# A stack of graph attention layers on one core: repeated scores by two DMAs through DRAM and a parametric relu, in place of a matmul and a VectorE pass

## The chip, the core and the metric

One core of a Trainium2 chip. Times are device microseconds of one execution of the whole program, launch not included; the profiled execution has its own time and its own span (first to last instruction). Lower is better.

## What is computed

128 independent graphs of 128 nodes with 512 features go through four layers, each a graph attention with residual and layer normalisation. All attention has the same core: a score per pair of nodes is the sum of a source term and a target term, a leaky relu of slope 0.2 is put on it, non-edges are masked, and a softmax over the source nodes weighs their features. Cut to what matters:

```python
# layer 0: one head
scores = leaky_relu(s_src[:, :, None] + s_dst[:, None, :] + attn_b[0], 0.2)
attn = softmax(where(adj + eye == 0, -inf, scores), axis=-1)
x = layernorm(x + attn @ x)

# layer 1: two stacked attentions, four heads of 256, then one of 512
def gat_layer(x, mask, W, a_src, a_dst, bias, concat):
    xl = (x @ W).reshape(B, N, H, F)
    e = leaky_relu(asrc[:, :, None, :] + adst[:, None, :, :], 0.2)
    attn = softmax(where(mask[..., None], e, NEG_INF), axis=1)
    out = einsum('bsdh,bshf->bdhf', attn, xl)     # heads concatenated, or their mean
    return out + bias
h = elu(gat_layer(x, mask, W1, ..., concat=True))
x = layernorm(x + gat_layer(h, mask, W2, ..., concat=False))

# layer 2: eight heads of 64;  layer 3: one head, elu of the output
```

Everything is float32. Each graph has six calls of the attention core: l0 (1 head), l1 (4), l2 (1), l3 in two halves (4 and 4), l4 (1), fifteen heads in all.

## The kernel before

A generator `graph(g, loaded)` issues the instructions of one graph and yields between steps. The loop at the end keeps a list of active graphs and advances each by one step per tick; a new graph starts every 10 ticks (`STAGGER`), so many graphs are under way at once, each in another layer. The tile framework then puts the instructions of each engine in an order of its own and adds the semaphores; on the engine they run in that order. So a step that waits holds up those of other graphs behind it on the same engine. Tiles come from rotating pools (three buffers each in the working pool, four for the score tile `z` and the transposed weights `pt`), PSUM from eight banks in rotation.

The attention core is `attend` (lines 155 to 215). With nodes on the partitions it needs, on every partition, the row of scores of the other nodes:

- GpSimd multiplies the identity by the column of scores (L160), which gives a diagonal matrix per head, `dg`.
- TensorE multiplies a matrix of ones by it (L167): `pd` in PSUM holds the row of scores on every partition.
- ScalarE adds the partition's own score as a bias and writes `z` to SBUF, one instruction per head (L177).
- VectorE forms the leaky relu as max(0.2 z, z) over all heads (L181), then subtracts per head from the mask and takes the row minimum (L187).
- ScalarE takes the exponential with the row sum (L194); VectorE inverts the sum (L200); TensorE transposes (L208); VectorE copies the transposed weights to SBUF as `pt` (L211).
- Only in l1 (`scaled=True`) GpSimd multiplies the weights by the inverse sums ahead of the transposes (L202).

Around l1: `xl`, the projected features, takes the layer's bias on its way out of PSUM (L305, VectorE, two halves of 512). The output of the four heads is made already transposed: for each of eight blocks of 128 features the weight operand is the block of `xl` and the moving operand the head's `pt` (L318, eight matmuls of 128 columns into two banks). ScalarE takes exponential and relu from each bank (L324, L325), VectorE joins them to the ELU, `hT` (L327). `hT` feeds the second attention's scores (L336) and projection (L344) as it is.

Other lines that the prediction names: L260 (score products of layer 0 on VectorE), L283 and L289 and L299 (copy of the transposed x1, score matmul, projection of l1), L353 (output of l2), L376 (projection of layer 2's heads), L392 (outputs of its halves), L398 (their scaling), L423, L425, L427 and L430 (minimum, exponential, combination and residual of the last ELU), L225 and L226 (GpSimd's part of the normalisation), L228 (its end), L285 (GpSimd, residual plus bias). L108 belongs to the set-up, which runs once. The inputs and the output go over SP's DMA queue, three transfers per graph; the weights come over ScalarE's queue at the start.

Of the kernel before, what the change touches and what calls it, by code (L numbers as in the profile page):

```python
# [8 lines left out]
F32 = mybir.dt.float32  # L9
I32 = mybir.dt.int32  # L10
AF = mybir.ActivationFunctionType
ALU = mybir.AluOpType
AX = mybir.AxisListType

P = 128
# [10 lines left out]
def tile_gat_stack(  # L26
# [117 lines left out]
    io = ctx.enter_context(tc.tile_pool(name="io", bufs=3))  # L144
    wk = ctx.enter_context(tc.tile_pool(name="wk", bufs=3))
    sm = ctx.enter_context(tc.tile_pool(name="sm", bufs=8))

    def load(g):
        xt = io.tile([P, F], F32, tag="x0", name=f"x0_{g}")
# [2 lines left out]
        nc.sync.dma_start(out=at, in_=adj[g])  # L152
        return xt, at

    def attend(g, lay, src, dst, mask, nh, res, scaled=False):


        n = f"{lay}_{g}"
        dg = wk.tile([P, 4, P], F32, tag="diag", name=f"dg_{n}")
        nc.gpsimd.tensor_mul(  # L160
            dg[:, :nh, :],
            ident.unsqueeze(1).to_broadcast([P, nh, P]),
            dst.unsqueeze(2).to_broadcast([P, nh, P]),
        )
        yield
        pd = bank(f"pd_{n}")
        nc.tensor.matmul(  # L167
            pd[:, : nh * P],
            lhsT=ones,
            rhs=dg[:, :nh, :].rearrange("p h j -> p (h j)"),  # L170
            start=True,
            stop=True,
        )
        yield
        z = wk.tile([P, 4, P], F32, tag="z", name=f"z_{n}", bufs=4)
        for h in range(nh):
            nc.scalar.activation(  # L177
                z[:, h, :], pd[:, h * P : (h + 1) * P], AF.Identity, bias=src[:, h : h + 1]
            )
        yield  # L180
        nc.vector.scalar_tensor_tensor(  # L181
            out=z[:, :nh, :], in0=z[:, :nh, :], scalar=SLOPE, in1=z[:, :nh, :],
            op0=ALU.mult, op1=ALU.max,
        )
        nm = sm.tile([P, 4], F32, tag="nm", name=f"nm_{n}")
        for h in range(nh):
            nc.vector.tensor_tensor_reduce(  # L187
                out=z[:, h, :], in0=z[:, h, :], in1=mask, scale=-1.0, scalar=FMAX,
                op0=ALU.add, op1=ALU.min, accum_out=nm[:, h : h + 1],
            )  # L190
        yield
        rs = sm.tile([P, 4], F32, tag="rs", name=f"rs_{n}")
        for h in range(nh):
            nc.scalar.activation(  # L194
                z[:, h, :], z[:, h, :], AF.Exp, bias=nm[:, h : h + 1], scale=-1.0,
                accum_out=rs[:, h : h + 1],
            )
        yield
        ri = sm.tile([P, 4], F32, tag="ri", name=f"ri_{n}")
        nc.vector.reciprocal(ri[:, :nh], rs[:, :nh])  # L200
        if scaled:
            nc.gpsimd.tensor_mul(  # L202
                z[:, :nh, :], z[:, :nh, :], ri[:, :nh].unsqueeze(2).to_broadcast([P, nh, P])
            )
            yield
        pp = bank(f"pp_{n}")
        for h in range(nh):
            nc.tensor.transpose(pp[:, h * P : (h + 1) * P], z[:, h, :], ident)  # L208
        yield
        pt = wk.tile([P, 4, P], F32, tag="pt", name=f"pt_{n}", bufs=4)  # L210
        nc.vector.tensor_copy(  # L211
            pt[:, :nh, :].rearrange("p h i -> p (h i)"), pp[:, : nh * P]
        )
        yield
        res.append((pt, ri))
# [26 lines left out]
    def graph(g, loaded):  # L242
# [53 lines left out]
        for c in range(2):  # L296
            px = bank(f"px1_{g}_{c}")
            for k in range(KF):
                nc.tensor.matmul(  # L299
                    px, lhsT=xT[:, k, :], rhs=w1t[:, k, c * 512 : (c + 1) * 512],  # L300
                    start=(k == 0), stop=(k == KF - 1),
                )

            cols = slice(c * 512, (c + 1) * 512)
            nc.vector.tensor_add(xl[:, cols], px, b1t[:, cols])  # L305
        yield
        yield from attend(g, "l1", sc1[:, H1:], sc1[:, :H1], m1, H1, res, scaled=True)
        pt, ri = res.pop()


        e1 = wk.tile([P, KH, P], F32, tag="e1", name=f"e1_{g}", bufs=2)
        r1 = wk.tile([P, KH, P], F32, tag="r1", name=f"r1_{g}", bufs=2)
        hT = wk.tile([P, KH, P], F32, tag="hT", name=f"hT_{g}", bufs=2)
        for c in range(2):
            pa = bank(f"pa1_{g}_{c}")
            for u in range(4):
                k = 4 * c + u
                nc.tensor.matmul(  # L318
                    pa[:, u * P : (u + 1) * P], lhsT=xl[:, k * P : (k + 1) * P],
                    rhs=pt[:, k * P // FH, :], start=True, stop=True,  # L320
                )
            yield
            cols = slice(4 * c, 4 * c + 4)
            nc.scalar.activation(e1[:, cols, :].rearrange("p k i -> p (k i)"), pa, AF.Exp)  # L324
            nc.scalar.activation(r1[:, cols, :].rearrange("p k i -> p (k i)"), pa, AF.Relu)  # L325
            yield
            nc.vector.scalar_tensor_tensor(  # L327
                out=hT[:, cols, :], in0=e1[:, cols, :], scalar=-1.0, in1=r1[:, cols, :],
                op0=ALU.add, op1=ALU.min,
            )  # L330
        yield


# [146 lines left out]
```

## Time and profile before

| | us |
|---|---|
| median of 3 runs | 4681.03 |
| lowest to highest | 4670.32 to 4681.74 |
| the profiled execution, its time | 4670.32 |
| the profiled execution, its span | 4668.5 |

| engine | busy us | share of the span | instructions |
|---|---|---|---|
| PE (matmuls) | 4325.3 | 93% | 18692 |
| PEld (weight loads, beside PE) | 2605.1 | 56% | 18692 |
| DVE (VectorE) | 3559.1 | 76% | 10952 |
| ACT (ScalarE) | 1928.9 | 41% | 6913 |
| POOL (GpSimd) | 1725.1 | 37% | 2566 |

The 16 DMA engines were busy for about 6% of the span, and the mean granted clock of TensorE was 0.977. The chain of work that ended last is made of TensorE for 43%, VectorE for 41%, GpSimd for 7%, ScalarE for 3%; 5% is issue.

How to read it: a matmul of float32 is two records in the trace. In the groups, the columns are line, engine, operation, out<-in by the program's names, shapes and count, then busy time, mean nanoseconds of one, and idle time ahead of it with what ended it. A name as `z_l` stands for the tile of all layers. "DVE", "ACT", "POOL" and "SP" are VectorE, ScalarE, GpSimd and SyncE. The shares of the whole span are means over 128 graphs in a pipeline; the figures per graph are what counts, and they are had by dividing by 128, or from windows in the steady stretch.

### The profile page before, as it was taken

What the parts mean: (1) busy time and instruction counts of PE and PEld (TensorE: products, weight loads), DVE (VectorE), ACT (ScalarE), POOL (GpSimd) and SP (SyncE); (2) the same over time, 40 slices, a digit from 0 to 9 for tenths busy, and PEclk for the clock granted to TensorE, in tenths of its full rate; (3) what the DMA queues carried; (4) which work ended last, traced back from release to release, by engine and by line L of the source; (5) the groups of instructions that cost most, each with busy time, mean ns of one, the idle gap of its engine ahead of it and who ended that gap; (6) DMA issues with size and microseconds to landing.
All of it is one profiled execution on the core that took longest, in us unless ns stands there. A gap on an engine that the chain in (4) does not pass through costs nothing.

```text
span 4668.5 us, 61210 instructions
## 1 busy us (share of the span) xinstructions
PE 4325.3 (93%) x18692; PEld 2605.1 (56%) x18692; DVE 3559.1 (76%) x10952; ACT 1928.9 (41%) x6913; POOL 1725.1 (37%) x2566
## 2 busy tenths in 40 slices
PE   1999999999999999999999999999999999999997
PEld 0555555555555555555555555555555555555554
DVE  5577777777777777777777777777777777777777
ACT  0344444444444444444444444444444444444443
POOL 1333333333333333333333333333333333333332
PEclk9999999999999999999999999999999999999998
DMA  2000000000000000000000000000000000000000
GB/s 89 9 16 19 16 18 18 16 16 18 19 16 18 19 16 18 18 17 18 19 17 16 18 19 16 18 19 16 18 18 17 16 18 19 16 18 19 16 10 16
DMA packets 63142, 88.15 MB, mean 19 GB/s; under 512 B 10816, under 2 KB 27200, under 8 KB 62816
## 3 DMA queue, kind: packets, MB, share of 16 engines
q1 hardware_dynamic: 55296, 75.52, 5.0%
q10 hardware_dynamic: 7520, 8.72, 0.6%
q8 instruction: 151, 2.47, 0.2%
q14 instruction: 175, 1.43, 0.1%
HBM read 50.66 MB, written 33.55 MB: 18 GB/s over the span
## 4 chain that ended last, share of the span: by engine, by line
PE 43%; DVE 41%; POOL 7%; issue 5%; ACT 3%; ACTq 0%; DMA 0%; POOLq 0%; SPq 0%; DVEq 0%
PE px L299 21%; DVE z_l L187 7%; PE pc L336 5%; DVE x L228 4%; DVE z_l L181 4%; DVE y L427 4%; DVE st_n L220 3%; DVE pt_l L211 3%; PE pp_l L208 3%; POOL rd_n L226 3%; PE pc L289 3%; POOL z_l L202 3%; PE pa L318 3%; PE pd_l L167 2%; PE pa L392 2%
## 5 line engine op out<-in xcount | busy, mean ns | idle before, releaser
L194 ACT ACTIVATE z_l<-z_l,nm_l 128x128 f32<-128x128 f32 x1920 | 765.3, 406 | 1083.1 <-DVE nm_l L187 1082.8
L299 PE MATMUL px<-w1t,x1T 128*128 128x512 f32 x2048 | 985.4, 638 | 0.0
L344 PE MATMUL px<-w2t,hT 128*128 128x512 f32 x2048 | 919.7, 602 | 0.0
L160 POOL TENSOR_TENSOR dg_l<-ident,sc 128x128 f32<-128x128 f32 (+1 forms) x768 | 663.0, 876 | 668.9 <-PE pd_l L167 394.1
L225 POOL TENSOR_SCALAR rd_n<-mv_n 128x1 f32<-128x1 f32 x512 | 116.1, 227 | 1735.4 <-DVE mv_n L222 1360.5
L187 DVE CUSTOM_DVE_ANT_0 z_l<-z_l,m 128x128 f32<-128x128 f32 x1920 | 673.9, 384 | 4.6
L299 PEld LDWEIGHTS px<-w1t,x1T 128*128 128x128 f32 x2048 | 405.5, 203 | 477.4 <-issue 477.4
L177 ACT ACTIVATE z_l<-pd_l,sc 128x128 f32<-128x128 f32 x1920 | 585.8, 378 | 162.0 <-PE pd_l L167 159.4
L344 PEld LDWEIGHTS px<-w2t,hT 128*128 128x128 f32 x2048 | 382.1, 192 | 432.6 <-issue 432.6
L167 PE MATMUL pd_l<-dg_l,ones 128*128 128x128 f32 (+1 forms) x1536 | 523.4, 436 | 14.8 <-POOL dg_l L160 14.8
L181 DVE SCALAR_TENSOR_TENSOR z_l<-z_l 128x128 f32<-128x128 f32 (+1 forms) x768 | 477.5, 622 | 5.8 <-ACT z_l L177 5.8
L376 PE MATMUL px<-wht,x2T 128*128 128x512 f32 x1024 | 471.0, 603 | 0.0
L228 DVE TENSOR_SCALAR x<-x,mv_n,rd_n 128x512 f32<-128x512 f32 x384 | 209.1, 545 | 320.4 <-POOL rd_n L226 320.4
L211 DVE COPY pt_l<-pp_l 128x128 f32<-128x128 f32 (+1 forms) x768 | 370.0, 482 | 84.5 <-PE pp_l L208 84.4
L305 DVE TENSOR_TENSOR xl<-px,b1t 128x512 f32<-128x512 f32 x256 | 176.5, 689 | 291.5 <-PE px L299 291.5
L194 ACT ACTIVATION_READ_ACCUMULATOR z_l<-z_l,nm_l 128x1 f32 x1920 | 385.4, 201 | 0.0
L208 PE MATMUL pp_l<-ident,z_l 128*128 128x128 f32 x1920 | 321.2, 275 | 18.7 <-ACT z_l L194 11.0
L289 PE MATMUL pc<-wc,x1T 128*128 128x8 f32 x1024 | 136.9, 260 | 210.5 <-ACT x1T L283 210.0
L324 ACT ACTIVATE e<-pa 128x512 f32<-128x512 f32 x256 | 153.1, 598 | 412.4 <-PE pa L318 412.4
L208 PEld LDWEIGHTS pp_l<-ident,z_l 128*128 128x128 f32 x1920 | 237.4, 145 | 124.4 <-issue 96.2
L226 POOL TENSOR_TENSOR rd_n<-rd_n,neghalf 128x1 f32<-128x1 f32 x512 | 291.7, 570 | 32.5
L392 PEld LDWEIGHTS pa<-xl,pt_l 128*128 128x128 f32 x2048 | 260.5, 193 | 66.0 <-issue 58.4
(78 smaller groups left out, 6449.6 us busy)
## 6 DMA issues: line engine op xcount, KB each, us to landing
x<-in_x_dram SPq DMA_DIRECT2D x128, 256.0 KB, 2.6
out_dram<-y SPq DMA_DIRECT2D x128, 256.0 KB, 2.0
adj<-in_adj_dram SPq DMA_DIRECT2D x128, 64.0 KB, 1.8
w1t<-in_L_gnn_W_dram ACTq DMA_DIRECT2D x1, 2048.0 KB, 11.2
w2t<-in_L_gnn_W_dram ACTq DMA_DIRECT2D x1, 2048.0 KB, 16.2
wht<-in_L_gnn_W_dram ACTq DMA_DIRECT2D x8, 128.0 KB, 5.5
b1t<-in_L_gnn_b_dram ACTq DMA_DIRECT2D x1, 512.0 KB, 6.3
a<-in_L_gnn_att_src_dram ACTq DMA_DIRECT2D x1, 512.0 KB, 5.6
```

The lines of the kernel that those rows point to most:

```text
L160: nc.gpsimd.tensor_mul(dg[:, :nh, :], ident.unsqueeze(1).to_broadcast([P, nh, P]), dst.unsqueeze(2).to_broadcast([P, nh, P]),)
L167: nc.tensor.matmul(pd[:, : nh * P], lhsT=ones, rhs=dg[:, :nh, :].rearrange("p h j -> p (h j)"), start=True, stop=True,)
L177: nc.scalar.activation(z[:, h, :], pd[:, h * P : (h + 1) * P], AF.Identity, bias=src[:, h : h + 1])
L181: nc.vector.scalar_tensor_tensor(out=z[:, :nh, :], in0=z[:, :nh, :], scalar=SLOPE, in1=z[:, :nh, :], op0=ALU.mult, op1=ALU.max,)
L187: nc.vector.tensor_tensor_reduce(out=z[:, h, :], in0=z[:, h, :], in1=mask, scale=-1.0, scalar=FMAX, op0=ALU.add, op1=ALU.min, accum_out=nm ...
L194: nc.scalar.activation(z[:, h, :], z[:, h, :], AF.Exp, bias=nm[:, h : h + 1], scale=-1.0, accum_out=rs[:, h : h + 1],)
L208: nc.tensor.transpose(pp[:, h * P : (h + 1) * P], z[:, h, :], ident)
L211: nc.vector.tensor_copy(pt[:, :nh, :].rearrange("p h i -> p (h i)"), pp[:, : nh * P])
L226: nc.gpsimd.tensor_tensor(out=rd, in0=rd, in1=neghalf, op=ALU.pow)
L299: nc.tensor.matmul(px, lhsT=xT[:, k, :], rhs=w1t[:, k, c * 512 : (c + 1) * 512], start=(k == 0), stop=(k == KF - 1),)
L344: nc.tensor.matmul(px, lhsT=hT[:, k, :], rhs=w2t[:, k, :], start=(k == 0), stop=(k == KH - 1))
L376: nc.tensor.matmul(px, lhsT=xT[:, k, :], rhs=wht[:, k].rearrange("p h o -> p (h o)"), start=(k == 0), stop=(k == KF - 1),)
```

## The change

`attend` no longer makes a diagonal matrix and multiplies it by ones. The column of scores of the nodes is written to a row in DRAM by one DMA and read back to all 128 partitions by a second, both on SP's queue; the second must wait for the first. The ScalarE instruction reads that tile in SBUF (with a step of the number of heads), adds the bias and applies the leaky relu in one instruction (Prelu with alpha 0.2). The VectorE pass is gone.

In l1 the weights are no longer scaled ahead of the transposes. The four heads' output is made with nodes on the partitions: the head's `pt` is the weight operand and 256 columns of `xl` the moving one. VectorE scales each head by its inverse sum and adds the bias, from PSUM; the ELU is taken on 1024 columns (minimum, exponential, combination); TensorE transposes the result in eight blocks, and ScalarE and VectorE copy one bank each to `hT`. `xl` leaves PSUM without bias, one half by ScalarE, one by VectorE.

```diff
+    dram = ctx.enter_context(tc.tile_pool(name="dram", bufs=4, space=bass.MemoryType.DRAM))
...
-    def attend(g, lay, src, dst, mask, nh, res, scaled=False):
+    def attend(g, lay, src, dst, mask, nh, res):
...
-        dg = wk.tile([P, 4, P], F32, tag="diag", name=f"dg_{n}")
-        nc.gpsimd.tensor_mul(
-            dg[:, :nh, :],
-            ident.unsqueeze(1).to_broadcast([P, nh, P]),
-            dst.unsqueeze(2).to_broadcast([P, nh, P]),
-        )
-        yield
-        pd = bank(f"pd_{n}")
-        nc.tensor.matmul(
-            pd[:, : nh * P],
-            lhsT=ones,
-            rhs=dg[:, :nh, :].rearrange("p h j -> p (h j)"),
-            start=True,
-            stop=True,
-        )
+        row = dram.tile([P, nh], F32, tag=f"row{nh}", name=f"row_{n}")
+        nc.sync.dma_start(out=row, in_=dst)
+        db = wk.tile([P, P, nh], F32, tag=f"db{nh}", name=f"db_{n}")
+        nc.sync.dma_start(
+            out=db.rearrange("p j h -> p (j h)"),
+            in_=row.rearrange("j h -> (j h)").partition_broadcast(P),
+        )
+        yield
         yield
         z = wk.tile([P, 4, P], F32, tag="z", name=f"z_{n}", bufs=4)
         for h in range(nh):
             nc.scalar.activation(
-                z[:, h, :], pd[:, h * P : (h + 1) * P], AF.Identity, bias=src[:, h : h + 1]
+                z[:, h, :], db[:, :, h], AF.Prelu, bias=src[:, h : h + 1], alpha=SLOPE
             )
         yield
-        nc.vector.scalar_tensor_tensor(
-            out=z[:, :nh, :], in0=z[:, :nh, :], scalar=SLOPE, in1=z[:, :nh, :],
-            op0=ALU.mult, op1=ALU.max,
-        )
...
-        if scaled:
-            nc.gpsimd.tensor_mul(
-                z[:, :nh, :], z[:, :nh, :], ri[:, :nh].unsqueeze(2).to_broadcast([P, nh, P])
-            )
-            yield
...
-            cols = slice(c * 512, (c + 1) * 512)
-            nc.vector.tensor_add(xl[:, cols], px, b1t[:, cols])
+            if c == 0:
+                nc.scalar.copy(xl[:, :512], px)
+            else:
+                nc.vector.tensor_copy(xl[:, 512:], px)
...
-            for u in range(4):
-                k = 4 * c + u
+            for u in range(2):
+                h = 2 * c + u
                 nc.tensor.matmul(
-                    pa[:, u * P : (u + 1) * P], lhsT=xl[:, k * P : (k + 1) * P],
-                    rhs=pt[:, k * P // FH, :], start=True, stop=True,
+                    pa[:, u * FH : (u + 1) * FH], lhsT=pt[:, h, :],
+                    rhs=xl[:, h * FH : (h + 1) * FH], start=True, stop=True,
                 )
             yield
-            cols = slice(4 * c, 4 * c + 4)
-            nc.scalar.activation(e1[:, cols, :].rearrange("p k i -> p (k i)"), pa, AF.Exp)
-            nc.scalar.activation(r1[:, cols, :].rearrange("p k i -> p (k i)"), pa, AF.Relu)
+            for u in range(2):
+                h = 2 * c + u
+                cols = slice(h * FH, (h + 1) * FH)
+                nc.vector.scalar_tensor_tensor(
+                    out=z1[:, cols], in0=pa[:, u * FH : (u + 1) * FH], scalar=ri[:, h : h + 1],
+                    in1=b1t[:, cols], op0=ALU.mult, op1=ALU.add,
+                )
+
+        nc.vector.tensor_scalar_min(t1, z1, 0.0)
+        yield
+        nc.scalar.activation(t1, t1, AF.Exp)
+        yield
+        nc.vector.scalar_tensor_tensor(
+            out=z1, in0=t1, scalar=-1.0, in1=z1, op0=ALU.add, op1=ALU.max
+        )
+        yield
+        for hT, pb, c in transposed(z1, KH, f"h1T_{g}", "hT"):
             yield
-            nc.vector.scalar_tensor_tensor(
-                out=hT[:, cols, :], in0=e1[:, cols, :], scalar=-1.0, in1=r1[:, cols, :],
-                op0=ALU.add, op1=ALU.min,
-            )
+            dst = hT[:, 4 * c : 4 * c + 4, :].rearrange("p k i -> p (k i)")
+            if c == 0:
+                nc.scalar.copy(dst, pb)
+            else:
+                nc.vector.tensor_copy(dst, pb)
```

More of the change, by code (lines that the diff above doesn't have):

```diff
@@ L302, in graph @@
                 )
-            cols = slice(c * 512, (c + 1) * 512)
-            nc.vector.tensor_add(xl[:, cols], px, b1t[:, cols])
+            if c == 0:
+                nc.scalar.copy(xl[:, :512], px)
+            else:
+                nc.vector.tensor_copy(xl[:, 512:], px)
         yield
-        yield from attend(g, "l1", sc1[:, H1:], sc1[:, :H1], m1, H1, res, scaled=True)
+        yield from attend(g, "l1", sc1[:, H1:], sc1[:, :H1], m1, H1, res)
         pt, ri = res.pop()
-        e1 = wk.tile([P, KH, P], F32, tag="e1", name=f"e1_{g}", bufs=2)
@@ L312, in graph @@
-        r1 = wk.tile([P, KH, P], F32, tag="r1", name=f"r1_{g}", bufs=2)
-        hT = wk.tile([P, KH, P], F32, tag="hT", name=f"hT_{g}", bufs=2)
+        z1 = wk.tile([P, HF], F32, tag="z1", name=f"z1_{g}", bufs=2)
+        t1 = wk.tile([P, HF], F32, tag="t1", name=f"t1_{g}", bufs=2)
         for c in range(2):
             pa = bank(f"pa1_{g}_{c}")
-            for u in range(4):
-                k = 4 * c + u
+            for u in range(2):
+                h = 2 * c + u
                 nc.tensor.matmul(
-                    pa[:, u * P : (u + 1) * P], lhsT=xl[:, k * P : (k + 1) * P],
-                    rhs=pt[:, k * P // FH, :], start=True, stop=True,
+                    pa[:, u * FH : (u + 1) * FH], lhsT=pt[:, h, :],
+                    rhs=xl[:, h * FH : (h + 1) * FH], start=True, stop=True,
```

## The prediction, made before the changed kernel ran

> **What bounds the kernel now.** I read the page's busy shares first, then busy time by windows, the waits, the groups by form, the timeline of TensorE and the chain that ended last.
>
> From the answer by windows (columns: length, then busy time and instructions of PE, PEld, DVE, ACT, POOL, then granted clock, DMA share, GB/s):
>
> ```profile
> 1000.00:2000.00 1000.00, 953.00 (x4135) 574.42 (x4134) 772.95 (x2403) 424.28 (x1525) 381.48 (x568) 0.98 0.06 17
> 2000.00:3000.00 1000.00, 951.30 (x4145) 574.54 (x4144) 775.83 (x2404) 424.17 (x1522) 380.48 (x565) 0.98 0.05 18
> 3000.00:4000.00 1000.00, 949.49 (x4117) 571.77 (x4116) 774.25 (x2417) 428.75 (x1542) 381.90 (x567) 0.98 0.06 18
> ```
>
> TensorE is busy 95.1% of the steady stretch. A graph has (18692 - 4)/128 = 146 of its records, so the 12397 records of these 3000 us are 84.9 graphs: one per 35.33 us, with 33.6 us of TensorE and 1.7 us of holes. VectorE follows with 27.4 us. So the kernel is bound by TensorE, and its holes are the second thing to look for. The waits name them:
>
> ```profile
> PE pc L289 <- ACT x1T L283: 210.0, 120, 1.8
> ```
>
> 210.0/128 = 1.64 us per graph: the first matmuls of layer 1 wait for the ScalarE copy of the transposed x1. Apart from one in the set-up, every other wait of PE in that list is below 20 us in total. The chain shows what that hole is the end of:
>
> ```profile
> 2523.85 0.60 DVE z_l L181
> ...
> 2539.73 1.44 DVE y L427
> 2541.17 0.60 DVE z_l L181
> 2541.77 0.60 DVE y L430
> 2542.64 0.28 issue
> 2543.11 0.47 ACT xl L381
> 2543.58 0.50 ACT x1T L283
> 2544.12 1.06 PE pc L289 x8
> ```
>
> For half of each period VectorE works without a pause and the chain runs through it; ScalarE's copy stands behind an exponential that waits for VectorE. L427 is to be noted: 1.44 us for 512 elements.
>
> [...]
>
> ```profile
> L427 DVE SCALAR_TENSOR_TENSOR y<-t,y x128: 681/1515/1517, 277.6 to 4661.8; 128x512 f32<-128x512 f32 x128
> ```
>
> (min/median/max in ns.) In the timeline the one of 1.44 us shown above runs beside a GpSimd L160 of 1087 ns. [...] The trace has one load of 1283 ns; the changed program as built also has just one, so parametric ReLU and exponential share a set.
>
> **The change, part by part, per graph.** Groups by form (busy us, mean ns):
>
> ```profile
> L160 POOL TENSOR_TENSOR dg_l<-ident,sc 128x512 f32<-128x512 f32 x384 | 452.9, 1180 | 115.6 <-DVE sc L294 103.2 <-DVE sc L373 6.5 <-DVE mv_n L222 4.8
> L181 DVE SCALAR_TENSOR_TENSOR z_l<-z_l 128x512 f32<-128x512 f32 x384 | 266.3, 694 | 1.3 <-ACT z_l L177 1.2
> L181 DVE SCALAR_TENSOR_TENSOR z_l<-z_l 128x128 f32<-128x128 f32 x384 | 211.1, 550 | 4.6 <-ACT z_l L177 4.6
> L187 DVE CUSTOM_DVE_ANT_0 z_l<-z_l,m 128x128 f32<-128x128 f32 x1920 | 673.9, 384 | 4.6
> ```
>
> TensorE is costed from start to start in its timeline, because its modelled ends overlap:
>
> ```profile
> 2518.15 0.60 PE L208 MATMUL pp_l<-ident,z_l 128*128 128x128 f32 x4
> 2518.58 1.02 PE L353 MATMUL pa<-xl,pt_l 128*128 128x512 f32 x2
> 2519.45 1.02 PE L167 MATMUL pd_l<-dg_l,ones 128*128 128x512 f32 x2
> ```
>
> - TensorE: the six broadcasts (L167) go: three of 512 columns at 0.86 us and three of 128 at 0.22 (two records of 0.11) = -3.24. Eight transposes of the layer-1 output come: 8 x 0.11 = +0.88. The head outputs (L318, 16 records of 0.11 = 1.78) become 8 records of 256 columns, half of 0.43 each = 1.72. Net -2.4.
> - VectorE: L181 goes, (266.3 + 211.1)/128 = -3.73. L305 and L327, two each at 0.69, -2.76. [...] L427 1.47 to 0.69, -0.78; L187, 15 x (384 - 285, what most of them take in the timeline), -1.49. New: four scalings from PSUM at 0.41 (L398, 256 elements) 1.62; the minimum of 1024, below twice L423's 0.41, 0.75; the ELU's 1024-wide combination 1.22 (L108 has that width[...]); two PSUM copies at 0.68. Sum +4.95. Net -3.8, to about 23.5 us.
> - ScalarE: fifteen biases stay as Prelu, from 0.378 to at most L194's 0.406 (SBUF source; a strided read of four heads is not shown by the trace: I take no surcharge, and bound it at double, 0.35 x 12 = 4.2, on an engine busy 15 us of 35). Two exponentials and two relus of 0.60 go; one 1024-wide exponential (1.06) and two copies (0.59) come: about zero.
> - GpSimd: L160 and L202 go, (663.0 + 133.7)/128 = -6.2 us[...].
> - SP: twelve more DMAs per graph at 0.34 us of issue (the out store's row) = 4.1 us beside three now. Each read must wait on SP for its row to land, and the DMAs behind it wait too: in the built order rows and reads stand in pairs (l2 with l0, l4 with l3's first half, l1 with l3's second), and the out store lies ahead of l1's read.
>
> Transfer times are bounded by these (KB, median us to landing):
>
> ```profile
> out_dram<-y SPq DMA_DIRECT2D x128, 256.0 KB, 2.0
> adj<-in_adj_dram SPq DMA_DIRECT2D x128, 64.0 KB, 1.8
> w0s<-in_L_gnn_attn_w_src_dram ACTq DMA_DIRECT2D x1, 256.0 KB, 3.5
> ac<-in_L_gnn_W_attn_dram ACTq DMA_DIRECT2D x2, 0.1 KB, 4.9
> ```
>
> A row of 4-byte pieces: 2.0 (a store) to 4.9 (single elements in the crowded set-up). A read: 1.8 for one head, 2.6 (the x load) to 3.5 for four, w0s being exactly one 2 KB row repeated on 128 partitions. I take 2.0 + 2.6.
>
> **What hides them.** I walked one period of the built TensorE order, zero at the end of layer 1's last projection. Until 3.5 come seven groups already fed (transposes, l2 and l0 outputs). Then l3's second half waits for VectorE, which first copies the projection and two attention tiles (1.2 us) and masks seven heads at 0.29 (to 3.25), then copies the tile (3.85): a hole of 0.5. Score matmuls and projection of layer 2 end at 14.0, outputs and transposes at 18.8, layer 3's scores and projection at 23.1, layer 1's scores at 24.0, its projection at 31.6. Against this:
> - l2: score at 5.5 to 7, landed by about 12, used by ScalarE at 14.6.
> - l4: score at 17.5, its read held on SP by l3's row until 20, landed by 22.6; used at 23.7, when the copy of layer 3's projection is through.
> - l1, the tightest: score 24.2, row landed 26.5, then the out store holds SP until about 28; landed near 31, used from 32.9.
>
> The 1.64 us hole closes: between the transposes of x1 and its scores now stand half the head outputs, layer 3's scores and projection, 5.2 us. So 33.46 us of TensorE (33.6 by the windows) - 2.42 = 31.04, plus the 0.5 hole, plus 0.55 that I allow for waits that the walk is too coarse for: 32.1 us, 3.23 less. Over 127 periods -410. Fill and drain, with too few graphs to cover a round trip, cost perhaps 7 more attentions of 3.5 us, +25. Span 4668.5 - 385 = 4283.5, and the 1.8 us between span and time of the profiled execution (4670.32) make 4285. That execution is 0.2% below the median, 4681; within the range.
>
> **The rivals.**
> - TensorE all but free of holes: 31.3 us, 4668.5 - 4.03 x 127 + 25 + 2 = about 4185. For it: VectorE keeps 8 us spare. Against: the 0.5 hole is in the order.
> - Round trips partly shown: the upper bounds, 4.9 + 3.5 to 4.1, bring l1's read in about 0.8 late and l4's 2 to 3: 33.3 us, about 4440. For it: SP is in order. Against: the upper rows are from the crowded set-up, the DMA share is 6%.
> - Slower: l1's read lands so late that its four heads hold ScalarE, then VectorE's masking, and with it the tile copy queued behind, for which TensorE waits. It is free until about 33, then a microsecond for a microsecond; it eats the gain when row and read together take about 11.7 us instead of 4.6. At 13 us the period is 36.6 and the time about 4860. Against: no row above comes near.
> - That the edit does less than it says: the built order has no L167 or L181 work left, so this is excluded.
>
> **How the numbers follow.** 0.3% is about what a measurement of this kernel can tell from no change. Forecast 0.62 (4230 to 4340), no holes 0.14, partly shown 0.14 (4340 to 4600), slower or level 0.10. Outside 4180 to 4470 lie about half of the second, a third of the third and the last: 0.2. Faster: the first three less a little, 0.87; within 0.3% 0.03; slower 0.10.
>
> **What would show it.** Right: spacing of graphs near 32 us, no wait of PE for the x1T copy, L427's successor near 0.69 us, VectorE near 23.5 us per graph, reads landing below 3.5 us. Wrong: ScalarE's Prelu waiting for a DMA of the repeated row by over 1 us per graph and PE idle before l3's output; or rows that need over 5 us.

## The result, and the profile after

| | median (range), us | against before |
|---|---|---|
| before | 4675.67 (4670.24 to 4681.74, 4 runs) | |
| after | 5408.89 (5403.92 to 5432.26, 4 runs) | 1.158 [1.154, 1.162] |

The change makes the kernel 15.8% slower; 4285 had been forecast. The profiled execution after took 5410.9 us, with a span of 5409.1.

First the same view by windows as before (length, then busy time and instructions of PE, PEld, DVE, ACT, POOL, then granted clock, DMA share, GB/s):

```profile
1000.00:2000.00 1000.00, 848.82 (x3331) 506.16 (x3331) 594.73 (x2066) 424.55 (x1320) 201.38 (x325) 0.89 0.19 40
2000.00:3000.00 1000.00, 835.82 (x3297) 499.71 (x3297) 589.31 (x2048) 422.01 (x1307) 197.45 (x318) 0.89 0.18 40
3000.00:4000.00 1000.00, 831.17 (x3292) 497.92 (x3290) 588.02 (x2029) 415.57 (x1296) 197.55 (x319) 0.89 0.19 39
```

TensorE is busy 84% instead of 95%, with fewer records to run (134 a graph instead of 146), and its granted clock fell from 0.98 to 0.89. VectorE, ScalarE and GpSimd have all come down or stand still: no engine has become the bound. From the start of one layer-1 projection to the next, which is called TensorE's period below, it is 40.62 us, 5.3 more than before.

Layers are counted by the attention calls here, as in the prediction: the scores, projection and outputs of layer 1 are L275, L285 and L302 of the kernel after, those of layer 2 (the model's second attention of layer 1) L335, L343 and L352, those of layer 3 (the model's layer 2) L367, L375 and L391. The waits say on what the time goes (us in total over 128 graphs, times, longest):

```profile
ACT z_l L172 <- DMA db_l<-row_l: 1088.6, 245, 17.6
...
PE pc L367 <- ACT x2T L363: 733.2, 122, 11.3
```

TensorE's wait for the x1T copy is gone. In its place the score matmuls of layer 3 (L367) wait 733.2/128 = 5.7 us per graph for the copy of the transposed x2, and ScalarE, which makes that copy, waits 8.5 us per graph for the repeated rows. SyncE's own list has the next step back:

```profile
SPq L164 <- DMA row_l<-sc: 1184.1, 430, 9.2
```

The chain that ended last, from 2516 to 2549 us, with what each piece took:

```profile
2516.82 0.17 DVE sc L340
2517.01 0.33 SPq L162
...
2517.39 8.70 DMA row_l<-sc
...
2526.16 4.06 DMA db_l<-row_l
...
2530.61 1.73 ACT z_l L172 x4
2532.34 0.48 ACT x2T L363
...
2532.86 1.89 PE pc L367 x8
2534.75 6.54 PE px L375 x8
2541.29 0.79 PE pc L275 x8
2542.08 6.97 PE px L285 x16
```

In place of VectorE's half of the period stands one round trip: the score of layer 2 (L340) is ready, its row takes 8.7 us to DRAM, the read back 4.1, and then the Prelus and, behind them in ScalarE's order, the copy for layer 3. TensorE in the same stretch (start, duration, and in brackets the idle time ahead):

```profile
2512.69 1.10 PE L391 MATMUL pa<-xl,pt_l 128*128 128x64 f32 x8 [0.58 <-DVE pt_l L197]
...
2526.62 1.03 PE L302 MATMUL pa<-xl,pt_l 128*128 128x256 f32 x4
2532.86 1.89 PE L367 MATMUL pc<-wc,x2T 128*128 128x16 f32 x8 [5.21 <-ACT x2T L363]
2534.59 6.70 PE L375 MATMUL px<-wht,x2T 128*128 128x512 f32 x8
```

Two things are to be seen. The hole of 5.21 us is there, and the eight records of the projection behind it (L375) take 6.70 us. In the kernel before the same eight (L376) took 3.68:

```profile
2499.47 3.68 PE L376 MATMUL px<-wht,x2T 128*128 128x512 f32 x8
```

TensorE runs at about half speed for a while. The view by windows, taken over this stretch of the kernel after, has a granted clock of 0.52:

```profile
2532.90:2541.00 8.10, 8.10 (x16) 4.38 (x17) 4.00 (x13) 3.24 (x9) 0.00 (x0) 0.52 0.20 41
```

The transfers (KB each, median us from issue to landing):

```profile
db_l<-row_l SPq DMA_DIRECT2D x384, 256.0 KB, 4.0
...
db_l<-row_l SPq DMA_DIRECT2D x384, 64.0 KB, 4.7
...
row_l<-sc SPq DMA_DIRECT2D x384, 0.5 KB, 7.9
row_l<-sc SPq DMA_DIRECT2D x384, 2.0 KB, 1.6
```

The smallest transfer is the slowest: a one-head row of 512 bytes takes 7.9 us, a four-head row of four times the bytes 1.6. And the three groups that the prediction spoke of (busy us, mean ns):

```profile
L172 ACT ACTIVATE z_l<-db_l,sc 128x128 f32<-128x128 f32 x1920 | 808.2, 491 | 1450.7 <-DMA db_l<-row_l 1088.6 <-PE pp_l L194 356.6 <-DVE z L310 4.3
...
L178 DVE CUSTOM_DVE_ANT_0 z_l<-z_l,m 128x128 f32<-128x128 f32 x1920 | 547.6, 299 | 450.8 <-ACT z_l L172 399.3
...
L426 DVE SCALAR_TENSOR_TENSOR y<-t,y 128x512 f32<-128x512 f32 x128 | 87.7, 685 | 0.8 <-ACT t L424 0.8
```

### The profile page after: what moved, and what is told of

It is laid out like the page before. It is cut to its first block, busy times and chain, and to the rows that moved or that the text cites. A ratio compares the mean times of both kernels' runs of the same rounds, so it can differ in the third digit from the quotient of the medians.

```text
span 5409.1 us, 58792 instructions
## 1 busy us (share of the span) xinstructions
PE 4380.4 (81%) x17156; PEld 2618.6 (48%) x17156; DVE 3126.1 (58%) x10696; ACT 2185.2 (40%) x6785; POOL 1026.7 (19%) x1670
## 4 chain that ended last, share of the span: by engine, by line
PE 46%; DMA 34%; ACT 12%; DVE 4%; issue 2%; SPq 1%; ACTq 0%; POOL 0%; POOLq 0%; DVEq 0%
DMA row_l<-sc 20%; PE px L285 16%; DMA db_l<-row_l 14%; PE px L375 13%; ACT z_l L172 11%; PE pc L367 4%; PE pc L335 4%; PE pa L391 3%; PE px L343 2%; PE pc L275 2%; DVE pt_l L197 2%; PE pp_l L194 1%; ACT x2T L363 1%; DVE z_l L178 1%; SPq L162 0%
## 5 line engine op out<-in xcount | busy, mean ns | idle before, releaser
L172 ACT ACTIVATE z_l<-db_l,sc 128x128 f32<-128x128 f32 x1920 | 808.2, 491 | 1450.7 <-DMA db_l<-row_l 1088.6
L343 PE MATMUL px<-w2t,h1T 128*128 128x512 f32 x2048 | 951.1, 608 | 0.0
L285 PE MATMUL px<-w1t,x1T 128*128 128x512 f32 x2048 | 912.1, 598 | 0.0
L367 PE MATMUL pc<-wc,x2T 128*128 128x16 f32 x1024 | 234.2, 369 | 733.2 <-ACT x2T L363 733.2
L178 DVE CUSTOM_DVE_ANT_0 z_l<-z_l,m 128x128 f32<-128x128 f32 x1920 | 547.6, 299 | 450.8 <-ACT z_l L172 399.3
L375 PE MATMUL px<-wht,x2T 128*128 128x512 f32 x1024 | 745.4, 895 | 0.0
L367 PEld LDWEIGHTS pc<-wc,x2T 128*128 128x128 f32 x1024 | 222.4, 319 | 782.8 <-ACT x2T L363 781.9
L285 PEld LDWEIGHTS px<-w1t,x1T 128*128 128x128 f32 x2048 | 380.0, 191 | 429.6 <-issue 429.6
L343 PEld LDWEIGHTS px<-w2t,h1T 128*128 128x128 f32 x2048 | 373.2, 192 | 373.2 <-issue 373.2
L375 PEld LDWEIGHTS px<-wht,x2T 128*128 128x128 f32 x1024 | 294.5, 302 | 348.0 <-issue 348.0
L391 PEld LDWEIGHTS pa<-xl,pt_l 128*128 128x128 f32 x2048 | 261.9, 194 | 207.4 <-DVE pt_l L197 147.6
L391 PE MATMUL pa<-xl,pt_l 128*128 128x64 f32 x2048 | 272.9, 277 | 78.1 <-DVE pt_l L197 78.1
L238 POOL TENSOR_SCALAR m<-adj 128x128 f32<-128x128 int32 x256 | 304.1, 1188 | 68.4 <-DVE nm_l L178 29.6
```

What stands on the lines that cost most here:

```text
L172: nc.scalar.activation(z[:, h, :], db[:, :, h], AF.Prelu, bias=src[:, h : h + 1], alpha=SLOPE)
L178: nc.vector.tensor_tensor_reduce(out=z[:, h, :], in0=z[:, h, :], in1=mask, scale=-1.0, scalar=FMAX, op0=ALU.add, op1=ALU.min, accum_out=nm ...
L238: nc.gpsimd.tensor_scalar(out=m, in0=a, scalar1=0.0, scalar2=-BIG, op0=op, op1=ALU.mult)
L285: nc.tensor.matmul(px, lhsT=xT[:, k, :], rhs=w1t[:, k, c * 512 : (c + 1) * 512], start=(k == 0), stop=(k == KF - 1),)
L343: nc.tensor.matmul(px, lhsT=hT[:, k, :], rhs=w2t[:, k, :], start=(k == 0), stop=(k == KH - 1))
L367: nc.tensor.matmul(pc[:, : 2 * H2], lhsT=xT[:, k, :], rhs=wc3[:, k, :], start=(k == 0), stop=(k == KF - 1),)
```

## The experiments

The theory: the one-head rows land late because they are made of 128 pieces of 4 bytes that lie side by side; l2's round trip is then longer than its cover, and TensorE pays twice, with a hole and with half speed after it. Rivals: the new head output moved the work that would have covered it; SyncE's queue is too full, so that transfers wait for the loads and the store; and the order alone is at fault, with the row's write and its read next to each other.

All times against the kernel before on the same chip (4669 to 4676 us there):

| kernel | us | ratio | TensorE's period, us |
|---|---|---|---|
| before | 4676 | | 35.34 |
| after | 5408.9 | 1.158 [1.154, 1.162] | 40.62 |
| e1 16-byte rows | 4587.9 | 0.980 [0.978, 0.983] | 34.64 |
| e2 4-byte rows, steps after the read | 6041.6 | 1.293 [1.291, 1.295] | 45.87 |
| e3 new head output alone | 4496.5 | 0.962 [0.961, 0.963] | 33.84 |
| e4 DMA and Prelu alone | 5613.0 | 1.201 [1.199, 1.203] | 42.33 |
| e6 Prelu alone | 4552.1 | 0.974 [0.972, 0.975] | 34.44 |
| e7 e6, scores as weights | 4568.7 | 0.977 [0.975, 0.979] | 34.42 |
| e8 after, with filler matmuls | 5689.8 | 1.217 [1.211, 1.223] | 42.93 |
| e9 after, loads and store from GpSimd | 5588.1 | 1.197 [1.194, 1.200] | 42.25 |
| e10 16-byte rows and a step | 4053.4 | 0.868 [0.866, 0.869] | 30.29 |
| e11 new head output and Prelu | 4485.8 | 0.961 [0.959, 0.962] | 33.92 |
| e12 e1, loads and store from GpSimd | 4444.6 | 0.951 [0.949, 0.953] | 33.41 |
| e13 4-byte rows and a step | 6015.9 | 1.289 [1.287, 1.291] | 45.75 |
| e15 DMA and Prelu alone, in e10's form | 4058.8 | 0.869 [0.868, 0.871] | 30.35 |

### e1: the rows in pieces of 16 bytes

```
+        if nh == 1:
+            four = sm.tile([P, 4], F32, tag="four", name=f"four_{n}")
+            nc.vector.tensor_copy(four, dst.to_broadcast([P, 4]))
+            dst = four
-        row = dram.tile([P, nh], F32, tag=f"row{nh}", name=f"row_{n}")
+        row = dram.tile([P, 4], F32, tag=f"row{nh}", name=f"row_{n}")
```

(and the tile of the read four wide for one head too.) Every row is now 2 KB, every read 256 KB.

> One-head rows are written as four copies, 16 bytes a piece, and read back as 2 KB rows. Late-row theory: the row lands in about 1.5 us in place of 8, the read in 4; from l2's score to its use there are 6.5 us, so TensorE's hole ahead of layer 3's scores falls from 5.2 to under 1 us, its half-speed stretch goes, and the time is 4250 to 4400. Queue theory (SP's order and its waits): 5300 to 5500, since no place in the queue changes. Load theory (bytes and packets slow every transfer): above 5400, as three reads per graph grow fourfold. Head-output theory (the new layer-1 output is the cost): about 5400.

It measured 0.980 [0.978, 0.983]: four times the bytes for one head, and 821 us less than the change. At 4588 us that is above the 4250 to 4400 of the late-row theory and far below what the rivals had. The longest wait of its TensorE, and its transfers:

```profile
PE pa L356 <- DVE pt_l L201: 326.4, 124, 3.8
```

```profile
db_l<-row_l SPq DMA_DIRECT2D x768, 256.0 KB, 4.5
...
row_l<-four_l SPq DMA_DIRECT2D x384, 2.0 KB, 2.4
row_l<-sc SPq DMA_DIRECT2D x384, 2.0 KB, 2.7
```

The row is down from 7.9 to 2.4 us, the wait ahead of layer 3's scores is gone, and a smaller hole of 326.4/128 = 2.5 us stands ahead of layer 2's outputs (L356). Slow records have moved there with it: the outputs behind a hole of 2.98 us took 2.08 us, behind one of 2.15 us 1.13. So the rows' form is most of the loss, but not all that stood between the change and its forecast.

### e2: more distance behind the read

Three more `yield`s after the read's issue, for one head, rows as in the change.

> The rows keep their 4-byte pieces, but one-head attentions take three more steps between the read's issue and its use. Late-row theory: rows still land in 8 us, but about 10 us more stand in front of the use, so the hole closes and the time is 4250 to 4450. Queue theory: over 5000, since SP's waits stay. Head-output theory: about 5400. Load theory: about 5400 if the engines are the limit.

It became slower still, 6042 us, and missed the 4250 to 4450 of the late-row theory; only the queue theory had allowed over 5000. SyncE stands 3549.9/128 = 28 us of each 46 us for rows to land, a one-head row now takes 9.6 us, and TensorE is idle 11.2 us per graph. So distance alone does not help while the rows are slow, and the wait for a row, which stands on SyncE and holds the transfers behind it, belongs to the account beside the length of one round trip.

### e3, e4, e6, e7, e11, e15: the parts alone

e4 is the kernel before with the DMA broadcast and Prelu; e3 is the change with the matmul broadcast and the VectorE leaky relu put back. e6 is the kernel before with

```
-                z[:, h, :], pd[:, h * P : (h + 1) * P], AF.Identity, bias=src[:, h : h + 1]
+                z[:, h, :], pd[:, h * P : (h + 1) * P], AF.Prelu, bias=src[:, h : h + 1],
+                alpha=SLOPE,
```

and without the leaky relu behind it.

> The matmul with the diagonal and the VectorE leaky relu come back, the new layer-1 head output stays. Late-row theory: no transfer left in the chain, TensorE 33.5 + 0.8 us per graph, so near the kernel before, 4650 to 4850, granted clock 0.97 to 0.98. Head-output theory: above 5200 with the hole ahead of layer 3's scores.

> Two DMAs and Prelu with the layer-1 head output of before (scaled weights, transposed output). Late-row theory: l2's row still lands in about 8 us, so TensorE has a hole of several us per graph and runs slowly after it: 5000 to 5450. Head-output theory: at or below 4680, since the part that costs is gone.

The head output is acquitted: alone it gains 3.8%, and the DMA part without it loses 20.1%, with the same hole. Neither time lies within the range of the late-row theory (e3 is below 4650, e4 above 5450), but both contradict the head-output theory:

```profile
PE pc L358 <- ACT x2T L354: 797.5, 128, 8.1
```

> The kernel before with Prelu straight from PSUM and no VectorE leaky relu: nothing else changes. VectorE loses 3.7 us of 27.4 per graph; the 1.64 us hole of TensorE ahead of layer 1's scores, which hangs on VectorE's chain, shrinks or goes. 4450 to 4600 if that hole is the only thing to gain (TensorE's 33.5 us stay), 4670 if the order puts another wait in its place.

Prelu alone is worth 2.6%. e7 goes one further and takes the score column, repeated with a step of 0, as the weights and the identity as the moving operand, so that GpSimd's diagonal goes:

```
+        for h in range(nh):
+            nc.tensor.matmul(
+                pd[:, h * P : (h + 1) * P], lhsT=dst[:, h : h + 1].to_broadcast([P, P]),
+                rhs=ident, start=True, stop=True,
+            )
```

> As the one before, and the row of scores is repeated with no diagonal: the column of scores, read with a step of 0, is the weight operand and the identity the moving one. GpSimd loses 5.2 us per graph[...]; TensorE's work for it stays about 3.3 us (15 matmuls of 128 columns, 0.22 each). 4380 to 4550. If weights with a step of 0 load slowly, the L167 counterpart goes above 0.22 each.

It takes GpSimd from 36% to 24% busy and TensorE's idle time from 1.28 to 0.19 us per graph, and yet gives 0.977 [0.975, 0.979], no better than e6 and just outside the expected range: the idle time went, and TensorE's own work grew by as much (layer 2's projection from 7.03 to 7.82 us, among others). The trace shows why that projection grew: in part of the graphs it runs at a granted clock of 0.50, though no hole over 0.19 us stands ahead of it (the lines are under e14).

> The other two parts without the DMA: the matmul broadcast stays, the new head output and the Prelu straight from PSUM are in. TensorE needs 33.46 + 0.88 - 0.06 = 34.3 us per graph and has no hole, so about 4490, as with the new head output alone (4496): Prelu then only empties VectorE, which doesn't bind. If VectorE still bound in that run, it falls to about 4400.

e11 is level with e3: TensorE is 97% busy in both, so what Prelu takes off VectorE (82% to 72%) is worth next to nothing there. The gains of e3 and e6 do not add: e3 has 0.12 us of idle time left per graph for Prelu to remove.

> The DMA part of the change alone in the form of e10 (16-byte rows, one step between row and read, Prelu), with the four-head output of the kernel before. The broadcasts gone are worth 3.24 us of TensorE per graph, so 33.46 - 3.24 = 30.2 us if no hole opens: about 4000 (3950 to 4200). If the new head output is what makes the cover for l2's round trip, a hole stays ahead of layer 2's scores and the time is above 4300.

The DMA part in its good form gains by itself all that the whole change in that form gains (0.869 against 0.868, with intervals that overlap). Its period of 30.35 us is 33.46 - 3.24 = 30.2, as worked out.

### e5: the transfers by themselves

Two kernels without the attention. In the first, sixteen transfers of each form were issued in a row, and the order that came out let up to five forms share the queue.

> Measures the transfers alone, one in flight at a time; all attention work is left out and the output is zeros. Late-row theory: a row of 128 pieces of 4 bytes side by side lands in about 8 us even on an idle queue, one of 16-byte pieces in about 1.5. If the pieces collide because several share one stretch of DRAM, then 8-byte pieces lie between (about 4), and pieces of 4 bytes with a pitch of 64 or 512 bytes land in 1.5 to 2.5, with a pitch of 16 in about 2. If the size of the piece alone counts, every 4-byte form takes about 8. Load theory (the transfers are slow because the queues are full): all of them land in 2 to 2.5 here. The repeated rows (512 B and 2 KB to 128 partitions) against plain loads of 64 and 256 KB: 3 to 4 against 1.8 and 2.6 if repeating one row is itself slow.

Rows whose pieces lie side by side, of 0.5 to 8 KB, all took 11.4 to 11.8 us there, and 4-byte pieces further apart 5.9. That is neither theory's figure; with several forms in flight at once they can't be told apart. The second kernel makes each transfer depend on the one before.

> The transfers one after another, each waiting for the one before, so that none shares the queue; attention is left out and the output is not the reference's. Shared-line theory: pieces of 4 bytes side by side about 8 us, of 8 about 4, of 16 about 1.5 to 2, of 32 and 64 about 1.5; 4-byte pieces at a pitch of 16 bytes like 16-byte pieces (about 2), at 64 and 512 bytes about 1.5. Piece-size theory: every 4-byte form about 8. Load theory: all about 2. Reads: the row of 512 B or 2 KB repeated on 128 partitions 3.5 to 4.5 against about 2 for a plain load of the same size, if repeating one row is slow by itself; equal if the crowded queue was the reason.

One at a time, on an empty queue (KB each, median us to landing; `four` to `sixtyfour` are 128 pieces of so many bytes side by side, `fourpitchsixteen` 128 pieces of 4 bytes at a distance of 16; `rep` is one row repeated on all partitions, `plain` a load of the same size without repeating):

```profile
rep_quad<-row_quad SPq DMA_DIRECT2D x8, 256.0 KB, 3.9
plainquad<-in_x_dram SPq DMA_DIRECT2D x8, 256.0 KB, 2.6
...
rep_one<-row_one SPq DMA_DIRECT2D x8, 64.0 KB, 4.6
plainone<-in_adj_dram SPq DMA_DIRECT2D x8, 64.0 KB, 1.7
...
four<-back_four SPq DMA_DIRECT2D x8, 0.5 KB, 7.1
...
eight<-back_eight SPq DMA_DIRECT2D x8, 1.0 KB, 2.9
...
sixteen<-back_sixteen SPq DMA_DIRECT2D x8, 2.0 KB, 1.4
...
sixtyfour<-back_sixtyfour SPq DMA_DIRECT2D x8, 8.0 KB, 1.4
...
fourpitchsixteen<-ack_fourpitchsixteen SPq DMA_DIRECT2D x8, 0.5 KB, 1.4
```

This settles the row. It takes 7.1 us with nothing beside it, so the load on the queue is not the cause. Nor is the size of a piece: the same 4-byte pieces, 16 bytes apart, take 1.4. It is that small pieces lie side by side; pieces of 8 bytes, at 2.9 us, stand between. 16-byte pieces, at 1.4, are as quick as 64-byte ones. Why small pieces side by side are slow is not shown by any run. The read has a cost of its own too: repeating one row takes 3.9 and 4.6 us where a plain load of that size takes 2.6 and 1.7.

### e8: useless matmuls in the hole

Five matmuls of 512 columns, whose result nobody reads, behind the transposes of x2.

> The changed kernel with five useless matmuls of 512 columns (4.3 us at full speed) behind the transposes of x2, where TensorE has its hole of 5.2 us; nobody reads them. If TensorE runs at half speed after an idle stretch, layer 3's score and projection records go back from 0.85 to 0.43 us start to start, the filler costs nothing, and the time falls by up to 3.3 us per graph, to 5000 to 5150. If the slow records have another cause (the DMAs, or power), they stay at 0.85 and the time stays at 5400 or rises.

The expected gain did not come: 5690 us, slower than the change. Layer 3's scores and projection are back at full speed (0.88 and 3.64 us, after 1.70 and 5.80), but idle time and slow records turn up elsewhere: per graph 2.4 us more on the transposes and 1.1 and 2.8 us more on layer 2's scores and projection than in the change. So filling the hole does bring back full speed behind it; but the reads are still late (ScalarE waits 1415.9/128 = 11.1 us per graph for them), and idle time opens elsewhere.

### e9 and e12: the queue relieved

The loads of x and adj and the store of the output issued from GpSimd, in the change (e9) and in e1 (e12).

> The changed kernel with the loads of x and adj and the stores of the output issued from GpSimd in place of SP, so that only rows and reads stand on SP's queue. Queue theory (rows held up by loads and stores that wait on SP): 4700 to 5100. Late-row theory: 5250 to 5500, since l2's row is issued right when its score is ready, and takes 8 us from there.

> Rows of one head in 16-byte pieces, with loads and stores of x, adj and the output issued from GpSimd. If what is left in the 16-byte version is SP standing before loads and stores (about 1.3 ms of waits on the span), 4250 to 4400; if it is the length of the round trip, 4500 to 4600.

With 4-byte rows this loses 3% more (5588, above both ranges), with 16-byte rows it gains 3% (4445, between the two ranges). The loads and the store on SyncE's queue are not what makes the change slow; once the rows are quick, an emptier queue is worth a little. In e9 SyncE still stands 2120.3/128 = 16.6 us per graph for rows, so this does not test what that wait costs.

### e10 and e13: a step between write and read

e10 is e1 with one `yield` between the row's write and its read, in every attention, so that SyncE does something else while the row lands. e13 is that step with the 4-byte rows. With the change and e1 they make a square.

> Rows of one head in 16-byte pieces, and one more step between row and read in every attention. If what is left in that version (2.7 us of TensorE holes per graph and slow records behind them) is the round trip still being too long for its cover, 4250 to 4450; if SP's queue or the order on VectorE holds it, 4550 to 4700 or worse.

> The changed kernel with its 4-byte rows kept, and one more step between the row's write and its read in every attention, as in e10. It is the fourth corner beside the change itself (5409), 16-byte rows (4588) and 16-byte rows with the step (4053). If the late landing of the 4-byte rows and what it makes SyncE's queue wait is the cause, the step has little to give: each 4-byte row still takes some 8 us and each read after it 4.6, and the read is issued later; well above 5000, probably 5300 to 6000, with SyncE waiting over 8 us a graph for rows. If it is the place of the read in the order alone, and the pieces matter little, at most 4700.

| us | write and read next to each other | a step between |
|---|---|---|
| 4-byte rows | 5409 | 6016 |
| 16-byte rows | 4588 | 4053 |

The step gains 535 us with quick rows, more than the 4250 to 4450 expected, and loses 607 with slow ones, about as expected, so it is no cure by itself, and the rows' form comes first. SyncE's wait for rows in e13:

```profile
SPq L165 <- DMA row_l<-sc: 2763.0, 583, 9.1
```

2763.0/128 = 21.6 us of 45.75, after 9.3 in the change. In e10 it is 4.0. That tells where e13's time goes, not why the step raises it; this stays open. e10, the fastest kernel here, has on its page:

```profile
PE 3909.9 (97%) x17156; PEld 2425.2 (60%) x17156; DVE 3311.2 (82%) x11080; ACT 2289.3 (57%) x6785; POOL 979.8 (24%) x1670
```

```profile
ACT z_l L177 <- DMA db_l<-row_l: 269.1, 214, 4.5
```

```profile
db_l<-row_l SPq DMA_DIRECT2D x768, 256.0 KB, 3.7
...
row_l<-four_l SPq DMA_DIRECT2D x384, 2.0 KB, 1.5
row_l<-sc SPq DMA_DIRECT2D x384, 2.0 KB, 1.6
```

TensorE has no hole left in the steady stretch. The step also moved the work: from the end of layer 2's projection to layer 3's scores TensorE now has 13.5 us of other work, the whole layer-1 projection among it, where the change had 4.9. So l2's round trip has its cover. How much of the gain is that and how much SyncE's freedom was not separated; issuing the reads from another queue than the rows was not tried.

### e14: does the hole itself bring half speed

Without the attention: groups of 16 matmuls (32 records of 512 columns), each released by a chain of ScalarE copies.

> The attention is left out; groups of 16 matmuls of 512 columns, each group released by a chain of 1, 3, 6, 9 or 14 ScalarE copies, so that TensorE stands still for about 1, 2, 4, 6 and 9 us ahead of them. If a hole itself brings the records of 853 ns that stand right behind holes in the changed kernel, then the first eight to ten records after the long idles (from somewhere between 2 and 5 us) are 853 ns, and those after the short ones 429. If the slow records come from something else (the operands' place, the copies beside them, the load on the whole chip), the records are 429 ns after all five.

The second round of five; the two others are like it, but for the first group of the program, which takes 15.72 us behind 2.79 us of idle at the start (start, length, idle time ahead):

```profile
103.34 14.00 PE L75 MATMUL out_none<-in_none,ident 128*128 128x512 f32 x32 [0.68 <-ACT in_none L70]
119.31 14.00 PE L75 MATMUL out_two<-in_two,ident 128*128 128x512 f32 x32 [1.97 <-ACT in_two L72]
137.23 16.77 PE L75 MATMUL out_four<-in_four,ident 128*128 128x512 f32 x32 [3.92 <-ACT in_four L72]
159.88 15.70 PE L75 MATMUL out_six<-in_six,ident 128*128 128x512 f32 x32 [5.87 <-ACT in_six L72]
184.69 16.94 PE L75 MATMUL out_nine<-in_nine,ident 128*128 128x512 f32 x32 [9.12 <-ACT in_nine L72]
```

After 0.68 and 1.97 us of idle the group takes 14.00 us, after 3.92 and more it takes 1.7 to 2.9 us longer, in each of the three rounds. From start to start, the first four to seven records behind a long idle take about 853 ns (eight to ten had been expected), the rest 429. So a long hole is enough by itself. In this run 1.97 us of idle costs nothing and 3.92 us does, the records come back to 429 ns, and the penalty does not grow with the idle time (2.77, 1.70 and 2.94 us; the rounds, 98.8 and 99.0 us apart, repeat each to within 0.1 us). In the second round the granted clock is 0.50 from 136.1 us on, 2.8 us after the last matmul of the group before (119.31 + 14.00).

In the kernels, though, half speed comes without such a hole too. In the kernel before, layer 1's projection behind the hole of 1.80 us takes 8.81 us, where the same sixteen records take 7.11 in e1 and e10. The granted clock is 1.00 over its first 0.9 us and 0.50 from 2510.5 to 2512.5 us, with TensorE busy throughout:

```profile
2507.70 1.06 PE L289 MATMUL pc<-wc,x1T 128*128 128x8 f32 x8 [1.80 <-ACT x1T L283]
2508.61 8.81 PE L299 MATMUL px<-w1t,x1T 128*128 128x512 f32 x16
```

And in e7 layer 2's projection takes 10.17 us, at a granted clock of 0.50, with no more than 0.19 us of idle time in the stretch ahead of it:

```profile
909.04 1.10 PE L380 MATMUL pa<-xl,pt_l 128*128 128x64 f32 x8 [0.19 <-DVE pt_l L199]
909.98 2.22 PE L324 MATMUL pc<-wc,hT 128*128 128x2 f32 x16
912.06 10.17 PE L332 MATMUL px<-w2t,hT 128*128 128x512 f32 x16
```

```profile
911.40:918.20 6.80, 6.80 (x13) 3.19 (x13) 3.67 (x12) 0.88 (x4) 1.79 (x3) 0.50 0.02 8
```

Here half speed stands behind 0.19 us of idle time, where e14 lost nothing behind 1.97. Ahead of that projection stand sixteen score records of only two columns (L324); in e3 and e10, whose granted clock is 0.994 and 0.992 in the mean (e7 0.967), they stand in two groups of eight with projection records between. Whether that makes the difference, no run here tests.

## Why the prediction was wrong, point by point

**The step that failed** is the transfer time: "A row of 4-byte pieces: 2.0 (a store) to 4.9", "I take 2.0 + 2.6". A one-head row measured 7.9 us (7.1 alone), above the upper bound too. The reads measured 4.7 for one head and 4.0 for four, where 1.8 and 2.6 had been read off plain loads, 2.6 was taken and 3.5 to 4.1 was the upper end. Only the four-head row was near what was taken (1.6 against 2.0). The neighbour chosen for the row, the output's store, writes long pieces and so says nothing about small ones side by side; the loads of single elements in the set-up had been put down to crowding. The signs that the prediction gave for being wrong are there: rows over 5 us, and Prelu waiting 8.5 us per graph for repeated rows.

**What followed from it.** The walk had l2's rows landed "by about 12", used at 14.6. In the trace the score came 8.5 us after layer 1's projection (forecast 5.5 to 7), and row and read took 8.7 + 4.1 = 12.8 us: 6.7 more than taken for the row, 1.5 for the read. With the forecast's 4.6 us they would have landed at about 2522 in the chain above, ahead of the end of x2's transposes at 2525.5; they landed at 2530.2. The copy for layer 3 stands behind the Prelu that waits, and TensorE behind the copy.

**The term that was left out.** Nothing in the sum was for TensorE's own speed behind a hole. It cost 0.83 + 2.28 = 3.11 us per graph on layer 3's scores and projection (1.70 and 5.80 against e10's 0.87 and 3.52), half as much as the hole. e14 shows that a hole of that length is enough for it (2.77 us lost behind 3.92 of idle, 1.70 behind 5.87), and e8 that the two are back at full speed when the hole is filled. The trace of the kernel before had the sign: 8.81 us on a projection behind its hole of 1.80, at a granted clock of 0.50 for part of it.

**The sum set right**, from start to start in the trace: e10's 30.29 us without holes; + 6.20 on layer 1's second outputs (7.93 against 1.73; the hole stands behind them); + 3.11 at half speed; + 0.80 on the transposes ahead of the 0.58 hole (2.44 against 1.64); + 0.20 on layer 2's and layer 3's outputs: 40.60, measured 40.62.

**TensorE's own work** was right: 31.04 forecast, 30.29 in e10. Of the 0.75 between them 0.60 was in the base: layer 1's projection took 7.55 us in the kernel before and 6.95 in e3, e10 and the change, where no hole stood right ahead of it. The one of 8.81 us under e14 has a granted clock of 0.81 over its length; that all of the mean's surplus is such half speed is an estimate from that one. The forecast of an almost hole-free kernel (4185 at 31.3 us) is what e10, with another form of row and another order, beats.

**VectorE** was right to 4%: 3126.1/128 = 24.4 us, 23.5 forecast.

**VectorE without GpSimd's L160 beside it** went as said: L427's 1467 ns became L426's 685, the masking's 384 became 299 (285 forecast). In e7, where the diagonal goes too, they are 682 and 284; in e6, where it stays, 1069 and 413.

**Prelu** needed no second table load, as said (one ACT_TABLE_LOAD of 1283 ns in the trace before and in the one after); a strided read was costed at no surcharge and measures 491 ns in the mean (one-head and four-head reads together; 517 in the median in e10, where all are strided) against at most 406: 15 x 0.085 = 1.3 us per graph, on an engine that has room.

**The holes.** The one of 1.64 us closed as forecast, and the new one ahead of layer 3's second outputs is 0.58 where 0.5 was worked out.

**The rivals.** The slower one had the mechanism (a late read holds ScalarE, and what is queued behind it holds TensorE) but put it at l1, "the tightest", and at the wrong queue: not VectorE's masking and tile copy but ScalarE's own next copy. At 13 us of row and read it gave a period of 36.6; measured at 12.8 us is 40.6, of which 3.1 is half speed. That the two lie no further apart is chance, since its price was worked out for l1's round trip and the wait is for l2's. Its chance of 0.10 rested on "no row above comes near".

## What to carry to other kernels

A transfer's time is read from a transfer of the same shape on both sides, and not from one of the same size: where no such row exists, its upper bound is open, and the forecast has to ask, for each round trip, at what value the sign turns. Here a broadcast through DRAM paid where rows were written in pieces of 16 bytes and the read was issued a step after the write: 13% (e10, and e15 without the new head output), while 4-byte pieces side by side lost 16 to 20% without the step and 29% with it. A hole on TensorE has to be costed with the half-speed stretch behind it, here 1.7 to 2.9 us more by itself from 3.92 us of idle time on, and 3.1 in the kernel. Shorter holes were not safe here (8.81 us instead of 7.11 behind one of 1.80): look in the trace of before for matmuls that take longer than the same ones elsewhere.

## What was not expected of the hardware

- 128 pieces of 4 bytes side by side in DRAM take 7.1 us to land, of 8 bytes 2.9, of 16 to 64 bytes 1.4; 4 bytes at a distance of 16, 64 or 512 bytes 1.4.
- Repeating one row on 128 partitions takes 4.6 us for 512 bytes and 3.9 for 2 KB; plain loads of the same total take 1.7 and 2.6. The shorter row is the slower to repeat.
- TensorE's records double from 429 to 853 ns behind an idle of 3.9 us and not behind 2.0, in a run of nothing but matmuls of 512 columns (e14); the loss, 1.7 to 2.9 us, does not grow with the idle time.
- In the kernels a granted clock of 0.50 also followed a hole of 1.80 us (before) and a stretch with no hole over 0.19 us (e7). What brings it there is not shown.
